# A mixture-of-experts pipeline over 66 of 68 slot tiles, the last two behind a branch

## The chip, the core and the metric

The kernel runs on one core of a Trainium2 chip. A core has five engines, each with its own stream of instructions: TensorE (PE, matrix products; its weight loads are shown apart as PEld), VectorE (DVE), ScalarE (ACT), GpSimd (POOL) and SyncE (SP), which here only issues transfers. ACT and POOL issue some transfers too. Sixteen DMA engines carry them between the chip's main memory and the core's on-chip memory (SBUF); products land in PSUM, a small accumulator memory in banks. Engines wait for each other by semaphores. The metric is the device time of one launch in microseconds (us); shorter is better.

## The reference

The input `x` has 2 sequences of 2048 tokens, 512 wide, all in float32. A normalized `xn` goes into causal attention with one head and into a mixture of experts (MoE); the result is `x + attention * silu(moe)`.

```python
xn = _layernorm(x)
s = attention(xn, qkv, o_proj, gamma, beta)      # normalizes again, causal softmax, + xn
# experts: 8 of them, each token uses its best 2
scores = xf @ gate_w.T + gate_b + bias
top_scores, top_idx = jax.lax.top_k(scores, 2)
gates = jax.nn.softmax(top_scores)
h = silu(xf @ w1[e].T + b1[e])                   # 512 -> 352
y = h @ w2[e].T + b2[e]                          # 352 -> 512
out = sum over the two experts of gate * y
x = x + s * silu(out)
```

There are 4096 tokens and so 8192 pairs of a token and an expert. How many of them each expert gets depends on the data.

## The kernel before

**Stages.** First the kernel folds the weights (`fold`), normalizes `x` block by block (`norm`, `keys`), and makes keys, queries and values, which it keeps in main memory. In the same stage `route` chooses the two experts of each token on VectorE. Then come the experts, tile by tile, and then attention, which gathers the experts' rows as it ends.

**Slots.** The experts work on slots of 128 rows, called tiles here. Each expert's tokens are laid out in halves of 64 rows; an expert with `n` tokens takes `n / 64` halves, rounded up. The number of tiles `NS` is fixed when the program is built, for the worst case that the data may bring: 8192 pairs and up to 63 rows of padding in each of 8 experts give 135 halves, so `NS` is 68. The first `FULL`, 60, are whole tiles of one expert each (52 of them in 26 pairs by `pair_step`, with fewer multiplications); the other 8 are half tiles, whose two halves may belong to different experts. `route` computes for each expert the halves that it uses, and sums them up over the experts in `behind`; its last element is the number of halves in use. Slots past that hold no pair. Nobody reads their rows of `y`, but the kernel computes them.

**One tile's chain.** For tile `i`: `gather` (POOL) reads the tile's rows of `zu_d` by index into `xs`; `turn` (a transposing transfer on SP) and `join` (DVE) make `xT`; `up` (PE) multiplies with `w1` into `ph`; `turn_h` scales it (ACT) into `h`, splits it (POOL) into `hu` and transposes it (SP) into `huT`; `join_h` (DVE, then ACT with the activation) makes `ht`; `down` (PE) multiplies with `w2` into `py`; `keep_y` copies it (DVE for these tiles) into one of two buffers `y` and stores it (SP) to the tile's rows of `y_d` in main memory. In a half tile PE works on 64 columns at a time, the two halves side by side; the second half's expert is copied into `w1c` (by ACT, `copy_w1`) and `w2c` (by DVE, `copy_w2`). Each such step reads an expert's number from SBUF into an engine's register.

**Order.** The order of the instructions on every engine is the order in which the program writes them, with no planner. `experts_step(i)` writes one step of the pipeline: the `y` of tile `i - 4`, the gather of `i + 6`, the transpose of `i + 4`, the join of `i + 1`, the up product of `i`, the down product of `i - 3`. The steps stretch over `i` from -5 to `NS + 4`. From step 59 on, each step also issues three parts of the list `early` on SP: 16 parts of the keys `k` and then 4 of the queries `q`, which the first scores of attention need, so the list ends in step 65. When it ends, POOL's `query_sums(0)` is written.

**Where experts end.** After step `NS - 1` the program writes:

```python
    copy_w2(NS - DOWN)
    for s in range(2):
        begin_scores(s)
    for j in direct(0):
        chunk_scores(0, j)
    for i in range(NS, NS + DOWN + 2):
        experts_step(i)
    st.close()
    wp.close()
```

`chunk_scores(0, j)` (PE, `ps`) is the first tile's work of attention, here between the last full step of the experts and the three down products that are left. `st.close()` and `wp.close()` give back the experts' buffers and weights; attention's own buffers are laid over them. Then the loop over attention's tiles begins: its first pass loads `v` (16 transfers on SP), makes `block_sums(0)` (`tk`, three parts on DVE and one on POOL), then the scores of the second tile (`ps`) and the products of `fast_scores` (`p`).

Of the kernel before, what the change touches and what calls it, by code (L numbers as in the profile page):

```python
# [12 lines left out]
I32 = mybir.dt.int32  # L13
# [7 lines left out]
P = 128  # L21
# [5 lines left out]
def gated_attention_moe(  # L27
# [28 lines left out]
    nc = tc.nc  # L56
    B, S, D = x.shape
    E, _, H = w1_t.shape
# [17 lines left out]
    FULL = (2 * NT * P - E * HALF) // P  # L76
    NS = -(-((2 * NT * P + E * (HALF - 1)) // HALF) // 2)
    NSP = NS + NS % 2
    NJ = FULL + 2 * (NS - FULL)
    assert HL < P and HL % 32 == 0 and D == 512 and TB == 512  # L80

# [19 lines left out]
    y_rows = y_d.rearrange("(n p) d -> p n d", p=P)  # L101

    const = ctx.enter_context(tc.tile_pool(name="const", bufs=1))
# [9 lines left out]
    share = [const.tile([P, 1, NT], F32, name=f"share{k}") for k in range(2)]  # L113
    toki = const.tile([P, NSP], I32, name="toki")
    eidi = const.tile([P, NJ], I32, name="eidi")
    b1sel = const.tile([P, NH, NJ], F32, name="b1sel")


# [46 lines left out]
    xin = {}  # L165
# [13 lines left out]
    nc.vector.memset(b1s, 0.0)  # L179
    gb = mp.tile([P, E, 1], F32, name="gb")  # L180
    gbias = mp.tile([P, E, 1], F32, name="gbias")

    def load_small():
        nc.sync.dma_start(out=gam, in_=gamma)
# [23 lines left out]
    def load_raw(c, pair):  # L208
        for i, queue in zip(pair, (nc.sync, nc.scalar)):

            cuts = (0, P, D) if c == 0 and i == 0 else (0, D)
            for at in (slice(*cut) for cut in zip(cuts, cuts[1:])):
                queue.dma_start(out=parts[i][:, c, at], in_=srcs[i][ts(c, P), at])
# [18 lines left out]
    def norm(b):  # L232
        norm_stats(b)
        norm_roots(b)
        norm_rows(b)
# [284 lines left out]
    def route():  # L520

        with ExitStack() as rt:
# [7 lines left out]
            for e in range(E):  # L530
# [5 lines left out]
                out=tri, in_=tri, compare_op=ALU.is_ge, fill=0.0,  # L536
# [105 lines left out]
            behind = rp.tile([P, 3, E, 1], F32, name="behind")  # L642
# [6 lines left out]

            shift = rp.tile([P, E, 1], F32, name="shift")
            nc.vector.scalar_tensor_tensor(
                shift, first[:, 0], float(HALF), excl[:, :, 0:1], ALU.mult, ALU.subtract
# [161 lines left out]
    load_small()  # L816
    for c in range(NK):
        load_raw(c, (2, 3))
    norm(0)
    fold(wqk, parts[0], parts[1], 1.0 / math.sqrt(KEY))  # L820
    keys(0)
# [59 lines left out]
    def gather(i):  # L881
        xs = xsp.tile([P, ZW], U16, name=f"xs_{i}", tag="xs")
        nc.gpsimd.indirect_dma_start(  # L883
            out=xs, out_offset=None, in_=zu_d,
            in_offset=bass.IndirectOffsetOnAxis(ap=toki[:, order[i] : order[i] + 1], axis=0),
        )
        xss[i] = xs
# [49 lines left out]
    DOWN = 3  # L937
# [13 lines left out]
    def turn(i):  # L951
        xh = xhp.tile([P, 2 * ND, P], U16, name=f"xhT_{i}", tag="xhT")
        nc.sync.dma_start_transpose(out=xh, in_=xss[i][:, : 2 * D])
        xhs[i] = xh

    def join(i):
        xT = xtp.tile([P, ND, P], F32, name=f"xT_{i}", tag="xT")
        nc.vector.tensor_copy(  # L958
            xT.bitcast(U16).rearrange("p c (t h) -> p c t h", h=2),
            xhs.pop(i).rearrange("p (h c) t -> p c t h", h=2),  # L960
        )
        xts[i] = xT
# [13 lines left out]
    def copy_w1(i):  # L976
        if i >= FULL:
            ev = expert(places(i)[1][1], mybir.EngineType.Activation)
            nc.scalar.copy(w1c, w1[0][:, bass.ds(ev, 1), :, :].rearrange("p o c h -> p (o c) h"))

    def copy_w2(i):
        if i >= FULL:
            ev = expert(places(i)[1][1], mybir.EngineType.DVE)
            for rows, c in ((P, slice(0, NH - 1)), (HL + 1, slice(NH - 1, NH))):
                nc.vector.tensor_copy(
                    w2c[:rows, c, :],
                    w2[:rows, bass.ds(ev, 1), c, :].rearrange("p o c d -> p (o c) d"),
                )

    def up(i):  # L990
        ev = experts[i] = expert(places(i)[0][1], mybir.EngineType.PE)
        xT = xts.pop(i)
        ph = ps_a.tile([P, TB], F32, name=f"ph_{i}", tag="a")[:, :H]
        for c in range(ND):
            rhs = [w1[0][:, bass.ds(ev, 1), c, :].rearrange("p o h -> p (o h)")]
            rhs += [w1c[:, c, :] for _ in places(i)[1:]]
            for k, (at, _) in enumerate(places(i)):
                nc.tensor.matmul(  # L998
                    ph[at, :], lhsT=xT[:, c, at], rhs=rhs[k],
                    start=(c == 0), stop=(c == ND - 1),  # L1000
                )
        phs[i] = ph
# [71 lines left out]
    def turn_h(i):  # L1074
        h = phs[i] if i in paired else hp.tile([P, H], F32, name=f"h_{i}", tag="h")
        nc.scalar.mul(h, phs.pop(i), xss.pop(i)[:, 2 * D : 2 * D + 2].bitcast(F32))
        hu = hus[i % NHU]
        nc.gpsimd.tensor_copy(  # L1078
            hu[:, :, :H], h.bitcast(U16).rearrange("p (d h) -> p h d", h=2)
        )  # L1080
        huT = hp.tile([P, 2 * NH, P], U16, name=f"huT_{i}", tag="huT", bufs=3)
        nc.sync.dma_start_transpose(out=huT, in_=hu.rearrange("p h d -> p (h d)"))
        huTs[i] = huT

    def join_h(i):
        ht = hp.tile([P, NH, P], F32, name=f"ht_{i}", tag="ht", bufs=3)
        nc.vector.tensor_copy(  # L1087
            ht.bitcast(U16).rearrange("p c (t h) -> p c t h", h=2),
            huTs.pop(i).rearrange("p (h c) t -> p c t h", h=2),
        )  # L1090
        for c, (h0, hn) in enumerate(HCH):
            for at, j in places(i):
                nc.scalar.activation(  # L1093
                    ht[:hn, c, at], ht[:hn, c, at], AF.Silu, bias=b1sel[:hn, c, j : j + 1]
                )
        hts[i] = ht

    def down(i):
        ht = hts.pop(i)
        ev = experts.pop(i)  # L1100
        py = ps_b.tile([P, D], F32, name=f"py_{i}", tag="b")
        for c, (_, hn) in enumerate(HCH):
            k = hn + 1 if c == NH - 1 else hn
            rhs = [w2[:k, bass.ds(ev, 1), c, :].rearrange("p o d -> p (o d)")]
            rhs += [w2c[:k, c, :] for _ in places(i)[1:]]
            for n, (at, _) in enumerate(places(i)):
                nc.tensor.matmul(  # L1107
                    py[at, :], lhsT=ht[:k, c, at], rhs=rhs[n],
                    start=(c == 0), stop=(c == NH - 1),
                )  # L1110
        pys[i] = py

    def keep_y(i, copy=nc.vector.tensor_copy):
        y = yp.tile([P, D], F32, name=f"y_{i}", tag="y")
        copy(y, pys.pop(i))  # L1115
        nc.sync.dma_start(out=y_rows[:, order[i], :], in_=y)
# [5 lines left out]
    def experts_step(i):  # L1122


        def at(f, k):
            if 0 <= i + k < NS:
                f(i + k)

        if i != NS:
            at(copy_w2, -DOWN)  # L1130
        if 0 <= i - DOWN - 1 < NS:
            keep_y(i - DOWN - 1, *[nc.scalar.copy] * (i < paired.start))
        if i >= 0:
            at(gather, FIRST)
        at(turn, 4)
        if i + 1 not in xts:
            at(join, 1)

        for _ in range((2, 2, 1, 4, 3, 3, 1)[i] if 0 <= i < paired.start else 0):
            w1_sums(*sums_left.pop(0))  # L1140
        if i < FULL:
            at(join_h, -2)
        at(up, 0)
        at(copy_w1, 1)
        at(turn_h, 0)
        if i >= FULL:

            at(join_h, -2)
        at(down, -DOWN)
# [165 lines left out]
    while w2_left:  # L1315
# [12 lines left out]
        out=keep, in_=keep, compare_op=ALU.is_ge, fill=-HUGE,  # L1328
        base=0, pattern=[[-1, P]], channel_multiplier=1,
    )  # L1330
    for i in range(NS):
        if i in paired:
            if (i - paired.start) % 2 == 0:
                pair_step(i)
            continue
        if i == paired.stop:

            pairs_st.close()
            right_st = lambda **k: right(reuse_waits="tile", **k)
            kp2 = right_st(st=att, name="kp2", bufs=NBB)  # L1340
            qp2 = right_st(st=att, name="qp2", bufs=NQ)
            sq = right_st(st=att, name="sq", bufs=1)


            wcp = right_st(st=st, name="wcp", bufs=1)
            w1c = wcp.tile([P, ND, H], F32, name="w1c")
            w2c = wcp.tile([P, NH, D], F32, name="w2c")
        experts_step(i)
        if i < paired.start:
            if i + 1 == paired.start:  # L1350
                join(i + 2)
                x_sums(i + 1)
        for _ in range(3):
            if i >= paired.stop and early:
                f, b, c = early.pop(0)
                f(b, c)
                if not early:
                    query_sums(0, nc.gpsimd)
    copy_w2(NS - DOWN)
    for s in range(2):  # L1360
        begin_scores(s)
    for j in direct(0):
        chunk_scores(0, j)
    for i in range(NS, NS + DOWN + 2):
        experts_step(i)
    st.close()
    wp.close()

# [471 lines left out]
```

## Time and profile before

| what | value |
|---|---|
| time, median of 3 runs | 1022.73 us (1021.96 to 1026.66) |
| the profiled execution's own time | 1024.79 us |
| its span, first to last instruction | 1023.1 us |
| busy: PE, DVE, POOL, ACT | 1013.5, 712.2, 482.1, 408.9 us |
| granted TensorE clock | 0.999 of full speed |
| half tiles: first up product, last down product starts | 525.4 us, 583.8 us |
| moved by DMA | 209.42 MB, mean 205 GB/s |

A line of the profile names an engine, the line of the kernel's file (L1107), the operation, the buffers written and read (`py<-arena,ht`), how many, and busy time, mean duration and the idle time before it with what ended it. In a listing by time the first number is the start in us from the span's start, the second the duration in us. A "q" behind an engine (SPq) means its queue of instructions that only issue transfers or handle registers. The chain that ended last is followed back from the last instruction: at each step to what released it, or to the instruction before it on its engine. Ends of matmuls are modelled, so a busy TensorE is not one at its peak.

### The profile page before, as it was taken

What the parts mean: (1) busy time and instruction counts of PE and PEld (TensorE: products, weight loads), DVE (VectorE), ACT (ScalarE), POOL (GpSimd) and SP (SyncE); (2) the same over time, 40 slices, a digit from 0 to 9 for tenths busy, and PEclk for the clock granted to TensorE, in tenths of its full rate; (3) what the DMA queues carried; (4) which work ended last, traced back from release to release, by engine and by line L of the source; (5) the groups of instructions that cost most, each with busy time, mean ns of one, the idle gap of its engine ahead of it and who ended that gap; (6) DMA issues with size and microseconds to landing.
All of it is one profiled execution on the core that took longest, in us unless ns stands there. A gap on an engine that the chain in (4) does not pass through costs nothing.

```text
span 1023.1 us, 13492 instructions
## 1 busy us (share of the span) xinstructions
PE 1013.5 (99%) x3956; PEld 666.2 (65%) x3956; DVE 712.2 (70%) x1395; ACT 408.9 (40%) x817; POOL 482.1 (47%) x479
## 2 busy tenths in 40 slices
PE   9999999999999999999999999999999999999998
PEld 4688888864666766676654447677675544447577
DVE  5777746896777777767734659778576556888667
ACT  3344445322454445444445222132345454542341
POOL 3364564003644444444431247164556776754272
PEclk9999999999999999999999999999999999999999
DMA  8799986989999999999999567454768769653371
GB/s 300 203 252 296 303 264 248 341 283 198 206 220 221 213 212 211 219 216 212 209 201 246 155 205 157 105 143 144 192 181 235 215 196 254 184 135 111 98 162 42
DMA packets 299367, 209.42 MB, mean 205 GB/s; under 512 B 234392, under 2 KB 247448, under 8 KB 298272
## 3 DMA queue, kind: packets, MB, share of 16 engines
q1 hardware_dynamic: 283840, 156.09, 61.7%
q0 software_dynamic: 10560, 35.17, 12.8%
q10 hardware_dynamic: 4896, 17.30, 4.6%
q8 instruction: 34, 0.56, 0.2%
q14 instruction: 37, 0.30, 0.1%
HBM read 92.89 MB, written 60.03 MB: 149 GB/s over the span
## 4 chain that ended last, share of the span: by engine, by line
PE 89%; DMA 4%; issue 3%; DVE 2%; POOL 1%; ACT 1%; SPq 1%; POOLq 0%; DVEq 0%; ACTq 0%
PE py L1107 15%; PE ps L1219 12%; PE p L1482 12%; PE p L1050 10%; PE p L1271 8%; PE po L1434 6%; PE bank_a L465 5%; PE bank_b L465 5%; PE bank_c L465 5%; PE p L1434 3%; PE bank_d L465 2%; PE ph L998 2%; DMA y_d<-y 1%; DMA raw<-in_qkv_t_dram 1%; PE pg L347 1%
## 5 line engine op out<-in xcount | busy, mean ns | idle before, releaser
L1107 PE MATMUL py<-arena,ht 128*128 (+3 forms) x408 | 182.3, 593 | 0.0
L1219 PE MATMUL ps<-k,q 128*128 128x512 f32 (+3 forms) x416 | 143.0, 495 | 0.0
L1394 POOL COPY pu<-pT 128x1024 uint16<-128x1024 uint16 (+2 forms) x74 | 82.5, 1147 | 119.4 <-ACT pT L1384 59.5
L1078 POOL COPY hu<-h 128x704 uint16<-128x704 uint16 x68 | 63.5, 953 | 154.6 <-issue 119.9
L1107 PEld LDWEIGHTS py<-arena,ht 128*128 128x128 f32 (+3 forms) x408 | 73.2, 183 | 82.1 <-issue 77.0
L1219 PEld LDWEIGHTS ps<-k,q 128*128 128x128 f32 x416 | 74.6, 190 | 66.8 <-issue 57.4
L883 POOL DMA_INDIRECT xs<-zu_d,toki x68 | 81.0, 1191 | 70.8 <-DVE toki L731 55.9
L1093 ACT ACTIVATE ht<-ht,b1sel 128x128 f32<-128x128 f32 (+3 forms) x228 | 71.1, 378 | 97.1 <-DVE ht L1087 97.1
L1057 DVE TENSOR_TENSOR h<-p,h 128x176 f32<-128x176 f32 x182 | 55.5, 337 | 60.8 <-PE p L1050 57.2
L1577 POOL DMA_INDIRECT yg<-y_d,posi x64 | 67.7, 1058 | 36.0 <-DVE yg L1588 20.5
L1434 PE MATMUL po<-v,pT 128*128 128x512 f32 x152 | 67.9, 593 | 0.4 <-DVE pT L1416 0.4
L280 POOL COPY zu<-z 128x1024 uint16<-128x1024 uint16 x32 | 37.5, 1173 | 61.3 <-DVE z L265 61.3
L1416 DVE COPY pT<-puT 128x1024 uint16<-128x1024 uint16 (+2 forms) x74 | 54.0, 757 | 10.3 <-DMA puT<-pu 10.2
L1384 ACT ACTIVATE pT<-pT,nm 128x1024 f32<-128x1024 f32 x14 | 16.1, 1148 | 110.2 <-DVE nm L1307 71.2
L1115 ACT COPY y<-py 128x512 f32<-128x512 f32 x55 | 32.2, 585 | 62.7 <-PE py L1107 48.1
L1384 ACT ACTIVATE pT<-ps,nm 128x512 f32<-128x512 f32 (+3 forms) x52 | 30.0, 581 | 64.5 <-DVE nm L1307 40.8
L1277 DVE TENSOR_TENSOR pT<-p,pT 128x512 f32<-128x512 f32 x49 | 32.9, 686 | 25.9 <-PE p L1271 22.2
L1434 PEld LDWEIGHTS po<-v,pT 128*128 128x128 f32 x152 | 28.5, 190 | 32.6 <-issue 30.9
L958 DVE COPY xT<-xhT 128x1024 uint16<-128x1024 uint16 x68 | 46.6, 709 | 4.3 <-DMA xhT<-xs 4.1
L1606 POOL TENSOR_TENSOR o<-o,yg 128x512 f32<-128x512 f32 x30 | 42.0, 1399 | 14.3 <-DVE o L1598 14.2
L1598 DVE SCALAR_TENSOR_TENSOR o<-xo,xscale,o 128x512 f32<-128x512 f32 x30 | 27.3, 918 | 28.7 <-ACT o L1595 28.7
L1087 DVE COPY ht<-huT 128x768 uint16<-128x768 uint16 x68 | 38.7, 569 | 10.3 <-DMA huT<-hu 10.2
(323 smaller groups left out, 2155.4 us busy)
## 6 DMA issues: line engine op xcount, KB each, us to landing
y_d<-y SPq DMA_DIRECT2D x68, 256.0 KB, 4.6
zu_d<-zu SPq DMA_DIRECT2D x32, 264.0 KB, 3.2
kt_d<-kT ACTq DMA_DIRECT2D x8, 1024.0 KB
k<-kt_d SPq DMA_DIRECT2D x32, 256.0 KB, 4.9
q<-qt_d SPq DMA_DIRECT2D x32, 256.0 KB, 5.3
v<-v_d SPq DMA_DIRECT2D x32, 256.0 KB, 4.7
xo<-in_x_dram SPq DMA_DIRECT2D x32, 256.0 KB, 4.0
x<-in_x_dram SPq DMA_DIRECT2D x30, 256.0 KB, 5.3
```

What stands on the lines that cost most here:

```text
L465: nc.tensor.matmul(ps[:, r, :], lhsT=lhs[:, c, ts(r, P)], rhs=rhs[:, c, :], start=(start and r + c == 0), stop=(c == 1), skip_group_check= ...
L883: nc.gpsimd.indirect_dma_start(out=xs, out_offset=None, in_=zu_d, in_offset=bass.IndirectOffsetOnAxis(ap=toki[:, order[i] : order[i] + 1], ...
L1050: nc.tensor.matmul(ps, lhsT=x[:, c], rhs=y(c).rearrange("p o h -> p (o h)"), start=(c == 0), stop=(c == ND // 2 - 1),)
L1078: nc.gpsimd.tensor_copy(hu[:, :, :H], h.bitcast(U16).rearrange("p (d h) -> p h d", h=2))
L1093: nc.scalar.activation(ht[:hn, c, at], ht[:hn, c, at], AF.Silu, bias=b1sel[:hn, c, j : j + 1])
L1107: nc.tensor.matmul(py[at, :], lhsT=ht[:k, c, at], rhs=rhs[n], start=(c == 0), stop=(c == NH - 1),)
L1219: nc.tensor.matmul(ps[:, :w], lhsT=aqs[seq[s] // 2][:, c, ts(t % 2, P)], rhs=aks[first + j][:, c, :w], start=(c == 0), stop=(c == ND - 1),)
L1271: nc.tensor.matmul(ps, lhsT=x[:, c], rhs=y[:, c], start=(c == 0), stop=(c == ND // 2 - 1))
L1394: nc.gpsimd.tensor_copy(pu[:, : 2 * w].rearrange("p (h d) -> p h d", h=2), turned[s][:, k : k + w].bitcast(U16).rearrange("p (d h) -> p h ...
L1434: nc.tensor.matmul(dst, lhsT=turned[s][:, ts(k, P)], rhs=avs[first + k // BT][:, k % BT, cols], start=(start and k == k0), stop=(k == k1 - 1),
L1482: nc.tensor.matmul(dst, lhsT=a[:, k], rhs=v(k), start=(k == 0), stop=(stop and k == n - 1))
L1577: nc.gpsimd.indirect_dma_start(out=y, out_offset=None, in_=y_d, in_offset=bass.IndirectOffsetOnAxis(ap=posi[k][:, n : n + 1], axis=0),)
```

## The change

The pipeline now runs over `NM = NS - 2`, 66 tiles. All four bounds that were `NS` in the expert steps are `NM`. Tiles 66 and 67 are written after the pipeline, each as a plain sequence of the ten steps of its chain, inside an `If`: the body runs when the number of halves in use exceeds `2 * NM`, 132. `route` copies that number as an integer to a new small tile, `used`, and every engine reads it into a register and branches on it. `fill_rows`, called early in the program, stores two blocks of `x` to the rows of `y_d` that belong to these two tiles, so that they hold something when the body is skipped.

```diff
+    NM = NS - 2
...
+    used = const.tile([P, 1], I32, name="used")
...
+    def fill_rows():
+        for k in range(NM, NS):
+            nc.sync.dma_start(out=y_rows[:, k, :], in_=xin[0][:, k - NM, :])
...
+            nc.vector.tensor_copy(used, behind[:, 2, E - 1])
...
     for c in range(NK):
         load_raw(c, (2, 3))
+    fill_rows()
     norm(0)
...
         def at(f, k):
-            if 0 <= i + k < NS:
+            if 0 <= i + k < NM:
                 f(i + k)
 
-        if i != NS:
+        if i != NM:
             at(copy_w2, -DOWN)
-        if 0 <= i - DOWN - 1 < NS:
+        if 0 <= i - DOWN - 1 < NM:
             keep_y(i - DOWN - 1, *[nc.scalar.copy] * (i < paired.start))
...
-    for i in range(NS):
+    for i in range(NM):
         if i in paired:
...
-    copy_w2(NS - DOWN)
+    copy_w2(NM - DOWN)
     for s in range(2):
         begin_scores(s)
     for j in direct(0):
         chunk_scores(0, j)
-    for i in range(NS, NS + DOWN + 2):
+    for i in range(NM, NM + DOWN + 2):
         experts_step(i)
+    n_used = nc.values_load(used[0:1, 0:1], min_val=0, max_val=2 * NS)
+    with tc.If(n_used > 2 * NM):
+        for i in range(NM, NS):
+            gather(i)
+            turn(i)
+            join(i)
+            copy_w1(i)
+            up(i)
+            turn_h(i)
+            join_h(i)
+            copy_w2(i)
+            down(i)
+            keep_y(i)
     st.close()
     wp.close()
```

## The prediction

> **What bounds the kernel now.** I read the page first, then the chain that ended last, then each engine in order of time around the change's place, the end of the experts (525 to 592 us).
>
> The page's busy row:
>
> ```profile
> PE 1013.5 (99%) x3956; PEld 666.2 (65%) x3956; DVE 712.2 (70%) x1395; ACT 408.9 (40%) x817; POOL 482.1 (47%) x479
> ```
>
> TensorE looks full, so two tiles fewer should be worth their matmuls. That is a mean over stages, so next comes the chain that ended last, in order of time, from 557 us (start us, us, what):
>
> ```profile
> 557.00 5.39 DMA y_d<-y
> 562.39 0.02 issue
> 562.42 0.69 DVE y L1115
> 563.11 0.61 DVE xT L958
> 563.72 0.04 issue
> 563.76 2.59 PE ph L998 x16
> 566.35 2.58 PE py L1107 x12
> 568.93 7.06 PE ps L1219 x16
> 575.99 8.42 PE py L1107 x36
> 584.41 6.21 PE ps L1219 x16
> ```
>
> Read backwards: the second score chunk (584.41) follows three down products (575.99), these follow the first tile's score chunks (568.93). Before 563.76 the chain leaves TensorE: the up product of tile 67 waits for `xT`, which stands on VectorE behind the copy of `y` of tile 62, which waits for the store of `y` of tile 60 to land (two `y` buffers). That store was issued only at 557.00, although its `y` was copied at 550.57 to 551.26. SyncE's queue was late. SP in order of time (start, us, line, what):
>
> ```profile
> 546.08 0.38 SPq L1116 DMA_DIRECT2D y_d<-y  x1
> 546.56 1.44 SPq L953 DMA_TRANSPOSE xhT<-xs  x1
> ...
> 551.68 1.50 SPq L953 DMA_TRANSPOSE xhT<-xs  x1
> ...
> 558.89 0.94 SPq L911 DMA_DIRECT2D k<-kt_d  x1
> 559.89 0.94 SPq L920 DMA_DIRECT2D q<-qt_d  x2
> ```
>
> SP carries, per tile, one `y` store, two transposes and three parts of the prefetch of keys and queries. The two `q` loads at 559.89 are the last things that the first score chunks need. GpSimd shows when they landed:
>
> ```profile
> 565.90 0.72 POOL L1238 TENSOR_TENSOR sq<-q 128x256 f32<-128x256 f32 x1 [8.22 <-DMA q<-qt_d]
> ```
>
> And the DMA engines are full there (window; busy by engine; clock, DMA share, GB/s):
>
> ```profile
> 535.00:545.00 10.00, 10.00 (x49) 4.00 (x49) 3.17 (x6) 5.47 (x13) 1.54 (x2) 1.00 1.31 204
> 545.00:555.00 10.00, 10.00 (x56) 5.02 (x54) 5.80 (x10) 5.80 (x17) 1.65 (x2) 1.00 1.08 283
> ```
>
> So up to about 557 the stage runs at TensorE's pace (half tiles start at 525.37, 530.66, 535.95, 541.24, 546.24, 552.0, 557.2, near 5.3 us apart, where ph and py alone are 2.59 + 2.58 = 5.17), but SP and the DMA engines follow close behind.
>
> [...]
>
> **The change part by part.**
>
> *Is the body skipped?* The reference's inputs give the experts 1037, 1102, 1013, 955, 1075, 976, 989 and 1045 of the 8192 choices; rounded up to halves of 64 that is 17+18+16+15+17+16+16+17 = 132. The test is "more than 132", so it is skipped. Expert 3 would need six more tokens to add a half.
>
> *Fill rows at the start.* Two stores of 256 KB on SP, each about 0.37 us to issue, at about 19.1 us, between the weights (17.25 to 19.10) and the `zu` stores (19.20). They wait for the first block of `x`, landed at 7.82 us. Behind them: the `zu` stores, then the load of block 2, which reuses the buffer read and so waits for the stores, some 4.6 us (the `y` row); issued about 24.5 instead of 21.5, landed about 30, read by VectorE at 37.99. SP's next work waits until 30.39 anyway. Cost 0; without that 8 us of cover, 3 us.
>
> *`used` copy.* One VectorE copy of 0.16 us (like `xscale`) in routing. TensorE runs without a gap over 226 to 251 us, so 0.
>
> *Removed, tiles 66 and 67.* On TensorE 2 x 5.17 = 10.3 us; between 557.0 (end of the down product beside tile 65) and 568.93, where the first score chunks start, lie these two steps and their stall: 11.9 us. On SP, transposes of `xs` 1.44 + 1.50 with gaps of 0.09, thus 3.1 us ahead of the `q` loads (the other four DMAs come after them). On POOL two gathers of 264 KB (526.4 and 530.9), copies `hu`; on ACT two w1 copies, `h`, the activations; on VectorE `xT`, `ht`, w2 copies, `y`: all off the chain once TensorE no longer waits there.
>
> *What is late next.* Without the two steps TensorE would start the score chunks at 557.0, but `q` landed at 565.8. The loads stay in step 64, and nothing is moved ahead for them. With 3.1 us less on SP they land at 562.7. Relief from the gathers and transposes can bring more; the floor is when the things ahead are ready: `h` of tile 64 at 551.62, `hu` to 552.5, its transpose to 553.9, three loads to 555.4, landing 5.4 later: 560.8. I take 561.7, so scores at 561.8 instead of 568.93: 7.1 us (ends 6.0 and 8.1). So some 4.8 us of the 11.9 become a new wait for `q`. The three down products behind keep their 8.42 us, since their waits on VectorE have the same order.
>
> *Register load and branch.* After the last down product each engine reads `used` into a register, and branches. The nearest row:
>
> ```profile
> L971 PEldq TENSOR_LOAD <-eidi x42: 295/357/1070, 243.1 to 559.7; - x42
> ```
>
> So 0.36 us on PE (to 1.07). [...] TensorE's sequencer runs ahead: that load at 559.7 serves tile 67, whose product starts at 563.76, and the last register operation of the down products was at 581.8, with the array busy to 584.4. So load and branch (about 0.5) fit under the last product. What the join costs is unknown[...]. If PE must run empty first, it restarts as at 584.34, where its weight loads stood 0.81 us before the first of `ps`; upper bound twice that, 1.6, lower bound 0. I take 0.7.
> Behind the branch: on VectorE `block_sums` (tk, 1.21 + 2.48 us, needed 9.5 us after the last down product, 593.89 against 584.41; slack 5); on POOL its part (2.34 us, before at 571.16, now after the join, since the buffers of the experts come free only there; needed 11 us after, so hidden); on SP the 16 loads of `v` (585.58 to 596.4, landing 5.9 later, first read at 612.46: slack 10 us); on ACT nothing for 8 us. So only TensorE's gap counts.
>
> *Sum.* 7.1 - 0.7 - 0.1 = 6.3 us. From 590 us on the chain is mostly TensorE's, so it carries to the end. The profiled execution took 1024.79 us, its span 1023.1, and 1.7 lie around it, unchanged; 1018.5 is what I expect of that execution. It stands 2.06 above the median, 1022.73, so 1016.4 for the median.
>
> **Rivals.**
> *A meeting of the engines at the branch.* All five wait for each other. The last is VectorE with the `y` copy (0.69), then SP with its store (0.4) and load and branch (0.5), then the signals there and back, ten steps of 0.05 (a semaphore step on PE takes 51 ns): 2.1 us, plus 0.7 to restart. Gain 4.2: about 1018.5. [...] Against: data waits suffice.
> *The join waits for the last `y` stores to land.* 0.69 + 0.4 + 4.6 + 0.5 + 0.7 = 6.9 us: gain 0.1, about 1022.6. With an instruction fetch on top, estimated at 1.0 (0.2% of 16 engines' span over 34 packets) to 4.6 (a store's landing), up to 1027. [...] Against: only SP and readers of `y` need them, and the first gather of `y` is at 614.2. To be slower by over 0.5% the branch must cost 12.3 us, so this needs several fetches in a row besides.
> *The branch is taken* (the change does not save what it says; slower). From 133 halves on both tiles run unpipelined: gather 1.2 + 5.0, transpose 1.4 + 4.6, `xT` 0.7, up 2.6, `h` 0.6, `hu` 0.8, transpose 1.4 + 4.6, `ht` 0.6, activation 1.5, down 2.6, `y` 0.7 = 28.3 us; the second, whose `xT` stands behind the first's `y` on VectorE, 16 more. Minus 6.3: about 1061. Against: the count above.
> *`q` is no limit.* The DMA relief pulls `q` in by 8 us: gain near 10.5, 1012. Against: the floor of 560.8.
>
> **How the numbers follow.** Likeliest case 0.62, its own range 1014.6 to 1017.6; meeting 0.16; landing wait 0.13, half of it above 1023; taken branch 0.03; `q` no limit 0.06. A difference under about 0.5% (5.1 us) can't be told from none by a measurement of this kernel: faster lies below 1017.6, slower above 1027.8. Faster: 0.62 less 0.06 at its edge, plus 0.06: 0.62. Slower: 0.03 and the landing wait's worst part, 0.06: 0.09. The rest, 0.29, is no difference. The range of 1014.0 to 1023.0 leaves out 0.06 below and about 0.10 above.
>
> **What the profile after would show.** Two gathers, two `y` stores and four transposes fewer, but two more `y` stores from `x` near 19 us; PE `ps` first at about 562, after a gap of some 5 us ended by DMA `q`; the three down products again 8.4 us; then a gap under 1.5 us before `ps` at about 578. A gap there of 3 us means the meeting, of 7 the landing wait; ph and py of tiles 66 and 67 after it would mean a taken branch. I am wrong if `q` lands at the old time, or the gap at the branch is over 2 us.

## The result, and the profile after

The kernel with the change took 1016.51 us in the median of 9 executions (1013.27 to 1019.85), the kernel before, on the same chip, 1022.99 (9 executions, 1021.96 to 1026.66). The ratio is 0.9935, with a 95% interval of 0.9916 to 0.9954: about 6.5 us, or 0.65%, faster. The prediction was 1016.4 us. The profiled execution of the change took 1013.27 us (span 1011.6) and was the lowest of its nine, while that of before (1024.79, span 1023.1) lay 1.8 us above its median. So the two profiles differ by 11.5 us where the medians differ by 6.5, and a part of what follows is about this difference.

The page's busy row of the changed kernel:

```profile
PE 1002.6 (99%) x3900; PEld 660.9 (65%) x3900; DVE 705.9 (70%) x1386; ACT 401.5 (40%) x801; POOL 473.0 (47%) x475
```

There are 56 products fewer on TensorE (3900 against 3956), which are the up and down products of two tiles, and it is busy for 10.9 us less. No instruction of tiles 66 and 67 was run. Where does the gain arise? From 21 us on, the starts of matching products of the two profiles agree within 0.02 us up to 548 us (in the first 21 us some differ by up to 0.65 us, which leaves no trace later), so the two stores of `fill_rows` and the copy of `used` cost nothing. What is left is the end of the experts. TensorE in order of time (as in the prediction: start us, duration us, what; in brackets the idle time before it and what ended it):

```profile
555.72 0.59 PE L1115 MATMUL py<-w2c,ht 97*64 97x512 f32 x1
557.91 7.11 PE L1227 MATMUL ps<-k,q 128*128 128x512 f32 x16 [1.60 <-issue]
...
573.73 6.25 PE L1227 MATMUL ps<-k,q 128*128 128x512 f32 x16 [0.30 <-PEq L1375]
```

The first score chunk starts at 557.91 instead of 568.93 us, 11.0 earlier, after a gap of 1.60 us. The second one, behind the three down products and the branch, starts at 573.73 instead of 584.41, 10.7 earlier. The difference of 0.3 is the gap at the branch. SyncE in order of time shows why the queries came so early:

```profile
546.99 1.22 SPq L1090 DMA_TRANSPOSE huT<-hu  x1
548.25 1.52 SPq L919 DMA_DIRECT2D k<-kt_d  x3
549.88 0.38 SPq L1124 DMA_DIRECT2D y_d<-y  x1
551.93 1.22 SPq L1090 DMA_TRANSPOSE huT<-hu  x1
553.20 0.57 SPq L919 DMA_DIRECT2D k<-kt_d  x1
553.82 0.94 SPq L928 DMA_DIRECT2D q<-qt_d  x2
554.86 0.41 SPq L1124 DMA_DIRECT2D y_d<-y  x1
```

In the kernel before, this queue issued one entry on the heels of the other, and `q` was issued at 559.89. Now it stands idle between a store and the next transpose (550.26 to 551.93): the backlog is gone, and `q` is issued at 553.82. The stores of `y` are early too: the two above are issued 2.0 and 2.1 us after their copies ended (547.84 and 552.78), against 5.7 for the one at 557.00 in the kernel before, and no wait for a store is left here. The DMA engines have a little more room (the same windows as in the prediction; the last three numbers are granted clock, DMA share and GB/s):

```profile
535.00:545.00 10.00, 10.00 (x49) 3.98 (x49) 4.46 (x8) 5.35 (x13) 1.55 (x2) 1.00 1.13 240
545.00:555.00 10.00, 10.00 (x60) 4.11 (x58) 5.61 (x9) 6.61 (x21) 2.82 (x3) 1.00 0.91 267
```

The shares fell from 1.31 and 1.08 to 1.13 and 0.91. GpSimd in order of time tells when the queries were all there, and when the branch was passed:

```profile
558.68 0.72 POOL L1246 TENSOR_TENSOR sq<-q 128x256 f32<-128x256 f32 x1 [3.46 <-DMA q<-qt_d]
...
573.66 2.35 POOL L1260 TENSOR_TENSOR tk<-k 128x1024 f32<-128x1024 f32 x1 [12.09 <-PEq L1375]
```

`sq` starts at 558.68 against 565.90. Its wait for `q` points to what ended TensorE's gap of 1.60 us, to which the list of TensorE puts only "issue"; the experiments below on the order of the loads show it. `tk` now stands behind the branch, as foreseen, and costs nobody time.

Last the branch itself. These are some of its instructions (durations in ns, least, median and greatest, then the start of the first and the last in us):

```profile
L1375 PEldq EVENT_SEMAPHORE  x2: 51/51/51, 573.5 to 573.6; - x2
...
L1375 POOLq COMPARE_BRANCH  x1: 45/45/45, 560.8 to 560.8; - x1
L1375 POOLq INC_SWDGE_SEM  x1: 1515/1515/1515, 561.8 to 561.8; - x1
...
L1375 ACTq COMPARE_BRANCH  x1: 45/45/45, 570.2 to 570.2; - x1
L1375 PEldq COMPARE_BRANCH  x1: 240/240/240, 571.8 to 571.8; - x1
L1375 DVEq COMPARE_BRANCH  x1: 72/72/72, 573.9 to 573.9; - x1
L1375 SPq COMPARE_BRANCH  x1: 53/53/53, 575.5 to 575.5; - x1
```

The engines pass it each at its own time: GpSimd at 560.8, ScalarE at 570.2, TensorE at 571.8, VectorE at 573.9, SyncE at 575.5. They don't meet. TensorE's sequencer branches while the array still works on the last down product, which ends at 573.43. Only the two semaphore steps at 573.5 and 573.6, of 51 ns each, come after it; what they are for the trace doesn't say. They leave the array idle for 0.30 us.

### The profile page after: what moved, and what is told of

It reads as the page before. It is cut to its first block, busy times and chain, and to the rows that moved or that the text cites. A ratio compares the mean times of both kernels' runs of the same rounds, so it can differ in the third digit from the quotient of the medians.

```text
span 1011.6 us, 13333 instructions
## 1 busy us (share of the span) xinstructions
PE 1002.6 (99%) x3900; PEld 660.9 (65%) x3900; DVE 705.9 (70%) x1386; ACT 401.5 (40%) x801; POOL 473.0 (47%) x475
## 5 line engine op out<-in xcount | busy, mean ns | idle before, releaser
L1115 PE MATMUL py<-arena,ht 128*128 (+3 forms) x396 | 176.7, 593 | 0.0
L891 POOL DMA_INDIRECT xs<-zu_d,toki x66 | 76.4, 1158 | 70.6 <-DVE toki L738 55.9
L1101 ACT ACTIVATE ht<-ht,b1sel 128x128 f32<-128x128 f32 (+3 forms) x216 | 68.0, 380 | 92.1 <-DVE ht L1095 92.1
L1628 POOL TENSOR_TENSOR o<-o,xo 128x512 f32<-128x512 f32 x30 | 43.2, 1439 | 2.4
```

Source lines behind the costliest of these rows:

```text
L891: nc.gpsimd.indirect_dma_start(out=xs, out_offset=None, in_=zu_d, in_offset=bass.IndirectOffsetOnAxis(ap=toki[:, order[i] : order[i] + 1], ...
L1101: nc.scalar.activation(ht[:hn, c, at], ht[:hn, c, at], AF.Silu, bias=b1sel[:hn, c, j : j + 1])
L1115: nc.tensor.matmul(py[at, :], lhsT=ht[:k, c, at], rhs=rhs[n], start=(c == 0), stop=(c == NH - 1),)
```

## The experiments

The theory: the two tiles' steps and their wait for `xT` leave TensorE, the loads of `q` come earlier because SyncE and the DMA engines have less to carry, and the rest of a wait for `q` remains; the branch costs little. The rivals: the gain is the work of the tiles alone and the transfers don't matter; the branch costs or brings something of itself; the two profiles differ by accident. The expectations were written down before each run.

**The change once more, unaltered.** No edit.

> The changed kernel once more, unaltered, to see what one execution's profile leaves out. Its first profiled execution took 1013.27 us and its span was 11.5 us shorter than before's, but the median of nine was only 6.5 us shorter. Theory (load timing): where the first score product starts varies from execution to execution with the landing of q; then a profile near 1016.5 us shows the gap ahead of it at 4 to 5 us instead of 1.6. Rival (clock): the granted clock falls for a few us in most executions (0.998 instead of 1.000 were listed); then the gap stays near 1.6 us and the loss of 2 to 6 us lies in a stretch at half clock elsewhere. Time 1014 to 1019 either way.

It took 1016.58 us (n = 6, 1014.05 to 1018.99), ratio 0.9936 (0.9915 to 0.9958). Neither expectation came true as written: the gap is neither 4 to 5 us nor 1.6, and the half clock that the rival looked for elsewhere follows the gap. Its profiled execution took 1016.66 us, right at the median, and is therefore the better witness of the usual case. TensorE in order of time:

```profile
559.59 8.80 PE L1227 MATMUL ps<-k,q 128*128 128x512 f32 x16 [2.43 <-issue]
...
577.11 6.25 PE L1227 MATMUL ps<-k,q 128*128 128x512 f32 x16 [0.30 <-PEq L1375]
```

The second score chunk starts 3.38 us later than in the other profile of the same kernel. Of these, 0.84 is a later last down product, 0.83 a longer wait (2.43 against 1.60), and 1.69 are the same 16 products, which took 8.80 instead of 7.11 us. The windows of this run (columns as above) say why:

```profile
557.00:560.00 3.00, 0.57 (x3) 0.30 (x2) 0.49 (x2) 0.00 (x0) 0.00 (x0) 1.00 1.23 301
560.00:563.00 3.00, 3.00 (x5) 1.32 (x4) 0.00 (x0) 0.00 (x0) 2.57 (x4) 0.52 0.81 210
```

Right after the gap the granted clock falls to half, for 3.41 us in all (from 560.1). A gap of 2.43 us was enough for that here, and one of 1.60 was not. The experiment that fills the gap, further down, says more on what counts.

How often does it happen? Of the 15 executions of the change in these two measurements, 11 had a mean granted clock of 0.998, with times of 1016.10 to 1019.85 us and a median of 1016.66. Four had 0.999 or 1.000, with times of 1013.27 to 1014.61. The first profile shows the rarer case. A mean clock over the execution doesn't tell where the half clock was; that it is at this place is shown in the profile of the second run only.

**Without the branch.** The register load, the branch and its body are removed. This kernel never computes tiles 66 and 67, which with these inputs hold no pair.

```diff
-    n_used = nc.values_load(used[0:1, 0:1], min_val=0, max_val=2 * NS)
-    with tc.If(n_used > 2 * NM):
-        for i in range(NM, NS):
-            gather(i)
...
-            keep_y(i)
```

> The changed kernel without the register load, the branch and its body (tiles 66 and 67 are never computed; with these inputs no pair lies in them). Theory (the join costs TensorE next to nothing): same time as the change within 0.5 us; the gap ahead of the second score chunk is 0.0 to 0.1 us instead of 0.30. Rival (the branch costs several us elsewhere, on VectorE, GpSimd or SyncE, which the profile of one execution hides): 2 to 5 us faster than the change.

1016.05 us (n = 22), ratio 0.9932 (0.9916 to 0.9948). The gap before the second chunk is gone:

```profile
559.08 8.55 PE L1227 MATMUL ps<-k,q 128*128 128x512 f32 x16 [2.61 <-issue]
...
575.98 6.28 PE L1227 MATMUL ps<-k,q 128*128 128x512 f32 x16
```

The branch is worth 0.5 us in the medians, within the uncertainty of both, and 0.30 in the traces. This execution too has a gap above 2.4 us followed by slow products (8.55 us).

**The branch alone.** The kernel before, all 68 tiles in its pipeline, with the copy of `used` and behind the pipeline the branch with its body, which is skipped.

```diff
+    NM = NS - 2
...
+    used = const.tile([P, 1], I32, name="used")
...
+            nc.vector.tensor_copy(used, behind[:, 2, E - 1])
...
+    n_used = nc.values_load(used[0:1, 0:1], min_val=0, max_val=2 * NS)
+    with tc.If(n_used > 2 * NM):
+        for i in range(NM, NS):
+            gather(i)
...
+            keep_y(i)
```

> The kernel before, all 68 tiles in the pipeline, and behind it the branch of the change, whose body would compute tiles 66 and 67 a second time and is not run. Theory (the join costs next to nothing): the time of before within 1 us, with a gap of about 0.3 us at the join. Rival (the branch costs 2 us or more, hidden in the change by the two tiles): 2 to 5 us slower than before.

1023.22 us (n = 22), ratio 1.0002 (0.9991 to 1.0012); the gap before the second chunk is the same 0.30 us. So the branch neither costs nor brings anything measurable, and the whole gain belongs to the 66 tiles.

```profile
567.13 7.13 PE L1222 MATMUL ps<-k,q 128*128 128x512 f32 x16
```

This profiled execution took 1022.95 us, near its median, and shows something of the kernel before too: at the end of the experts TensorE goes through all 68 tiles without a wait, the last two tiles' products fill 557.15 to 567.13, and the stall ahead of tile 67 in the profile of before (1.40 us of idle array) isn't there.

**The transfers kept.** The gathers and the first transposes of tiles 66 and 67 stay in the pipeline. Everything else of the change is as it was: no products, copies or stores of these tiles.

```diff
-        def at(f, k):
-            if 0 <= i + k < NM:
+        def at(f, k, end=NM):
+            if 0 <= i + k < end:
                 f(i + k)
...
-            at(gather, FIRST)
-        at(turn, 4)
+            at(gather, FIRST, NS)
+        at(turn, 4, NS)
...
-            gather(i)
-            turn(i)
             join(i)
```

> The change, with the two gathers and the first two transposes of tiles 66 and 67 left in the pipeline, and only the rest of the two tiles behind the branch. Theory (these transfers held up SP and the DMA engines, and their removal, not only that of the matmuls, moved q from 565.8 to 558.6 us): q lands at 561 to 565 us, TensorE waits 4 to 8 us for it, and the time is 3 to 7 us above the change. Rival (SP was late for other reasons, such as the y stores or the activations of tiles 66 and 67): q lands before 559.5 us and the time is that of the change within 1 us.

1023.75 us (n = 22, 1021.01 to 1028.09), ratio 1.0002 (0.9989 to 1.0016). The whole gain is gone, although TensorE has the products of two tiles less to do. Its waits (total us, times, longest), and the place in order of time:

```profile
PE ps L1227 <- DMA q<-qt_d: 6.8, 1, 6.8
```

```profile
563.19 9.97 PE L1227 MATMUL ps<-k,q 128*128 128x512 f32 x16 [6.76 <-DMA q<-qt_d]
...
581.88 6.25 PE L1227 MATMUL ps<-k,q 128*128 128x512 f32 x16 [0.30 <-PEq L1375]
```

The loads of `q` are issued at 558.05 instead of 553.82, and TensorE waits 6.76 us for them. Then it runs at half clock (windows of this run):

```profile
558.00:565.00 7.00, 1.81 (x2) 0.84 (x3) 0.00 (x0) 0.20 (x1) 1.00 (x2) 0.55 1.06 237
565.00:569.00 4.00, 4.00 (x6) 1.69 (x5) 0.00 (x0) 0.00 (x0) 1.81 (x3) 0.50 0.29 91
569.00:580.00 11.00, 11.00 (x41) 4.72 (x41) 6.57 (x12) 3.09 (x12) 0.00 (x0) 1.00 0.13 48
```

The half clock lasts 10.24 us here, three times 3.41. Against the first profile of the change the second chunk is 8.15 us later: 5.28 from the start of the first chunk and 2.86 from its slow products. By the medians the change lost 7.2 us, just above the expected 3 to 7, which had no term for the clock; the profiled execution (1021.30) was one of the lower ones of its 22. The theory of the transfers is shown: without their removal the tiles' work on TensorE turns into waiting.

**The gathers alone kept.** Of the edit above only that of the gathers, so that `turn` stays in the body.

```diff
-            at(gather, FIRST)
+            at(gather, FIRST, NS)
...
-            gather(i)
             turn(i)
```

> The change with only the two gathers of tiles 66 and 67 left in the pipeline (264 KB each on GpSimd's queue), their transposes behind the branch. With gathers and transposes left in, q was issued at 558.05 instead of 553.82 us and the first score product started at 563.2 instead of 557.9. Theory of the prediction (SP's own time for the two transposes, 3.1 us, is the larger part; the gathers are the smaller): q issued at 554.5 to 556, first score product at 558.5 to 560.5, time 0 to 3 us above the change. Rival (the gathers load the DMA engines and stretch all other transfers, so they are the larger part): q issued after 556, first score product after 561, 3 us or more above the change.

1017.08 us (n = 5, 1016.43 to 1022.20), ratio 0.9930 (0.9906 to 0.9954): 0.6 us above the change, within its uncertainty. The profiled execution was the longest of the five and had lost 3.7 us before this place, so its trace says little on the size. In it `q` is issued at 559.24, 3.7 less of which is 555.6, within the expected range, but the wait for `q` is 4.59 us and the first chunk takes 9.37. By the medians the gathers are the smaller part of the 7.2 us, though the intervals leave room for some 3 us; the rest comes with the two transposes, which stand in SyncE's own queue ahead of `q`. The transposes without the gathers were not run, since they need the gathered rows.

**The queries first.** In the change, only the order of the prefetch list: the keys and queries of the first tile's scores come first. Nothing is added or removed.

```diff
-    early = [(fetch_k, b, c) for b in range(NBB) for c in range(ND)]
-    early += [(fetch_q, n, c) for n in range(NQ) for c in range(2)]
+    early = [(fetch_k, b, c) for b in (2, 3) for c in range(ND)]
+    early += [(fetch_q, 0, c) for c in range(2)]
+    early += [(fetch_k, b, c) for b in (0, 1) for c in range(ND)]
+    early += [(fetch_q, 1, c) for c in range(2)]
```

> The change with the 20 prefetch parts in the order of use: keys 2 and 3, the first queries, keys 0 and 1, the second queries (as many transfers, same steps). Theory (a late q leaves TensorE idle for 1.6 to 2.8 us, and in most executions the idle time makes the clock fall to half for a window of 3.41 us, which costs 1.7 us more): no gap ahead of the first score chunk, no half clock but at the end, and 2 to 5 us less than the change: about 1011 to 1013 us, with less spread. Rival (the half clock has nothing to do with the gap, and the spread comes from elsewhere): the gap goes, half clock and spread stay, 1.5 to 2.5 us less than the change at most.

1012.55 us (n = 5, 1012.13 to 1014.83), ratio 0.9892 (0.9870 to 0.9913). SyncE issues the two loads at 540.92 and 544.25 us, and TensorE goes on without a gap and at full clock:

```profile
557.88 7.13 PE L1229 MATMUL ps<-k,q 128*128 128x512 f32 x16
...
573.73 6.25 PE L1229 MATMUL ps<-k,q 128*128 128x512 f32 x16 [0.30 <-PEq L1377]
```

The same kernel was measured again among the last runs:

> The change with the prefetch in the order of use once more, beside the filler on the same chip. Theory (no wait, so no half clock): 1012 to 1015 us, 1 to 2 us below the filler's lower group, whose extra products take 1.7 us of which the wait hides most.

1013.85 us (n = 6, 1012.26 to 1016.62), ratio 0.9901 (0.9880 to 0.9922), again with no gap before the first chunk. Of the 11 executions of this kernel ten had a mean granted clock of 1.000 and one 0.999. Their median is 1013.28 us, 3.2 below that of the 15 executions of the change (not on the same chip; by the ratios to the kernel before it is 3.5 to 4.5): about the wait (1.6 to 2.4) and the half clock (1.7) together. This version beats both kernels. The interval of the first of its two measurements lies just below that of the change, that of the second overlaps it.

**The transfers kept, the queries first.** The fourth kernel's edit and this order together.

> Gathers and first transposes of tiles 66 and 67 left in the pipeline, as in the run that lost the whole gain, but with the prefetch in the order of use (queries third of five groups instead of last). Theory (the transfers cost time only because they make q late): most of the loss returns, 1012 to 1015 us, no wait for q over 1 us. Rival (the transfers also delay y stores, keys and transposes, and with them the steps): still 1019 us or more.

1014.21 us (n = 6, 1012.00 to 1016.76), ratio 0.9912 (0.9893 to 0.9932). TensorE doesn't wait for `q`:

```profile
558.95 7.13 PE L1229 MATMUL ps<-k,q 128*128 128x512 f32 x16
```

Of the transfers' 7.2 us (1023.75 against 1016.51) nothing measurable is left: 0.4 us above the second measurement without them, 1.7 above the first. They cost time only because `q` stood behind them.

**The order in the kernel before.** The same four lines in the kernel before.

> The kernel before with only the prefetch in the order of use, all 68 tiles in the pipeline. There q landed at 565.8 us and was used at 568.93, and the stage waited for y stores. Theory (q is not what the kernel before waits for): within 1 us of before. Rival (the order of the prefetch is worth time by itself): 3 us or more faster than before.

1024.57 us (n = 14), ratio 1.0008 (0.9997 to 1.0019). The profiled execution was the slowest of the fourteen (1026.24). Its waits of TensorE still have the old one, now ahead of tile 66:

```profile
PE ph L1000 <- DVE xT L960: 1.6, 1, 1.6
```

With 68 tiles `q` is not what ends last. In this execution the up product of tile 66 waits, behind a store of `y`; in that of the branch alone TensorE waits for nothing at this place. So the order is worth some 3 us only once the tiles are gone. The two steps do not simply add.

**The branch taken.** The test is changed so that 132 halves pass it, and the body runs.

```diff
-    with tc.If(n_used > 2 * NM):
+    with tc.If(n_used > 2 * NM - 1):
```

> The change with the test one half lower, so that the 132 halves of these inputs take the branch and tiles 66 and 67 are computed behind it, unpipelined. The prediction's rival gives 28.3 us for the first tile and 16 for the second, 44 us above the change, about 1061 us. If the body overlaps more than that estimate allows (gathers and transposes of the second tile beside the first), 25 to 35 us above it.

1058.46 us (two executions, 1057.28 and 1059.63), ratio 1.0336 (1.0304 to 1.0368), so 42 us above the change; between the profiles 44.0 (1055.6 against 1011.6). Its waits of TensorE:

```profile
PE py L1115 <- ACT ht L1101: 12.5, 3, 6.7
PE ph L1006 <- DVE xT L966: 10.8, 2, 6.0
```

The body's chain is laid bare, and of its up and down products most run at half clock (0.79 us each for up, against 0.46). The sum of the prediction's rival fits, its parts less: the first tile takes 23.4 us (to the end of its `y` copy at 598.3, from the last down product at 574.9) instead of 28.3, since GpSimd, past the branch early, issues its gather already at 563.19, beside the down products, and the second takes 20.2 instead of 16. That is the price in a launch whose data fill 133 halves.

**Filling the gap.** Two products that nobody reads are written ahead of the first chunk, so that TensorE is not idle while it waits for `q`.

```diff
+    fill = ps_a.tile([P, TB], F32, name="fill", tag="a")
+    for _ in range(2):
+        nc.tensor.matmul(fill, lhsT=ident, rhs=w2[:, 0, 0, :], start=True, stop=True)
     for j in direct(0):
         chunk_scores(0, j)
```

> The change with two needless products of 512 columns (about 1.7 us of matmuls, result unread) ahead of the first score chunk, where TensorE waits for q. q is as late as before. Theory (idle time lowers the clock): idle time shrinks to about 1 us or nothing, the clock stays whole, and although TensorE does more work the kernel is 1 to 2 us faster than the change, near 1015 us or below. Rival (only q's lateness counts): the time of the change, or up to 0.5 us more.

> The two needless products ahead of the first score chunk once more, since the first time its six executions fell into two groups (1014.5 to 1014.8, 1017.7 to 1020.4) and the one profiled was slow for another reason, a stall near 290 us. Theory (idle time lowers the clock): no half clock after the wait for q, and the lower group again near 1014.6. If the half clock comes after it all the same, keeping TensorE busy is not what keeps the clock.

1016.22 us (n = 6, 1014.50 to 1020.35), ratio 0.9925 (0.9900 to 0.9949), and in the second measurement 1017.02 (n = 6, 1015.20 to 1020.10), ratio 0.9933 (0.9912 to 0.9955). Neither is apart from the change. The trace of the second:

```profile
561.84 1.98 PE L1372 MATMUL fill<-arena,ident 128*128 128x512 f32 x4
564.45 7.11 PE L1227 MATMUL ps<-k,q 128*128 128x512 f32 x16 [0.63 <-PE fill L1372]
```

At this place the filler did what was meant: from the end of the last down product (561.9) to the first score lie 2.5 us, as in the second run of the change (2.43), but the 16 products then take 7.11 us, not 8.80, and the clock stays full. The first filler trace shows the same. From the last down product to the second chunk both take 18.4 us, against 20.0 in the second run of the change. That the fall of the clock follows from the idle array, and not from the time or the transfers, is thus seen in both.

In the times the expected 1 to 2 us below the change did not appear; by them alone the rival fits as well, and the first measurement's lower group, 1014.5 to 1014.8, did not come back. Both profiled executions (1020.35 and 1019.88) lost 5 to 6 us elsewhere, near 290 us. One transpose of `xs` takes 4.7 and 5.7 us of SyncE's queue there, against 2.5 in the first profile of the change, TensorE waits 2.20 and 2.17 us, and a half clock of 3.41 us follows here too. Why the transpose took so long was not found.

All the traces together tell more about what counts. In each of the 14, every stretch of full or half clock that ends within the execution is a whole number of steps of 3.41 us (the full clock of 1017.17 us in the profile of before is 298 of them, that of 1006.93 in the first of the change 295), so the trace can be cut into such windows. The time that TensorE was idle within one window at full clock, and the clock of the next:

| profile | window, us | idle, us | next |
|---|---|---|---|
| the change, first | 555.03 to 558.45 | 1.60 | full |
| the branch taken | 555.73 to 559.14 | 1.77 | full |
| filler, second, near the end | 1012.88 to 1016.29 | 1.97 | full |
| without the branch | 555.17 to 558.59 | 2.12 | half |
| filler, second, near 290 us | 289.25 to 292.67 | 2.17 | half |
| filler, first, near 290 us | 292.24 to 295.66 | 2.20 | half |
| the change, again | 556.69 to 560.10 | 2.43 | half |

No window at full clock in the 14 traces goes against this: up to 1.97 us idle the clock stayed, from 2.12 us on it fell. The gap with the branch taken is 2.01 us long, but 0.24 of it lies in the next window. Whether it was spared by that or by its length can't be told from these runs.

## Why the prediction was right or wrong

The number was right, 1016.4 against 1016.51, and so was the mechanism: two tiles' work leaves TensorE, `q` comes earlier but becomes the next wait, and the branch costs little. Several terms of the sum were mis-sized or missing, and that they cancel to 0.1 us is luck.

*The body is skipped.* Right; and since the body runs when the test is one half lower, the halves in use are just the 132 that were counted.

*Fill rows and the `used` copy cost nothing.* Right: from 21 us on the starts agree within 0.02 us up to 548 us, and the branch alone with the copy gave 1.0002.

*The two tiles and their stall leave TensorE.* Right: all of that stretch is gone, and the wait for `xT` with it. The stretch was taken too long. The down product beside tile 65 ended at 557.23 us, not at 557.0, which makes it 11.7; and 1.40 of that was a stall which the profile of the branch alone, near its median, doesn't have. There the two tiles fill 10.0 us.

*The three down products keep their 8.42 us.* Right: from the end of the first chunk (565.0) to the end of the last product (573.4) it is 8.4.

*`q` is what is late next.* Right in kind: the order with the queries first takes exactly this wait away, and gains 3 us. Wrong in size: the step "a new wait of some 4.8 us". Measured were 1.6 and 2.4 us in the two profiles. The floor of 560.8 us was too high. In it, `h` of tile 64 was set at 551.62, its time in the kernel before; with less on SyncE it was ready at 550.71. The transpose was done at 553.15 instead of 553.9 and the loads were issued by 554.76 instead of 555.4. The landing was put at 5.4 us after that, the duration of the loaded stage; GpSimd had all of the `q` that it needs (558.68) after 3.9. And TensorE started 0.8 us before that, at 557.91. So the first chunk came 9.3 to 11.0 us earlier, not 7.1. How much the relief of the gathers would bring was the author's estimate; kept alone, they took 0.6 us by the medians. The error of method: the floor was built from times of a stage whose load the change itself removes.

*The missing term.* The prediction had the wait cost its own length. An idle array of 2.4 us also brought the half clock, which cost 1.7 us in the profile at the median. Wait and clock together are 4.1 us there, close to the 4.8 that the wait alone was given. The closeness of the result rests on this too.

*The sum.* Between the profile of before (1024.79) and the second of the change (1016.66) lie 8.1 us, where 6.3 were foreseen for this pair. In the traces they are 9.3 at the first chunk, less 1.7 of half clock and 0.3 at the branch, thus 7.3 at the second chunk, and 0.8 after it. The medians differ by 6.5 only, since that profile of before lay 1.8 above its median. Its stall ahead of tile 67 is probably a part of these 1.8. Counted from the profile of the branch alone, the first chunk comes 7.5 us earlier (567.13 to 559.59): 10.0 of the two tiles, less a wait of 2.4. Less the half clock of 1.7 it is 5.9 at the second chunk. So the prediction removed some 2 us too many and left out 1.7 of clock; against that it gave the new wait 2.4 us too many and the branch 0.4. The 0.1 in its sum belongs to no term that it names, and its worst landing wait, 1027, ends below the 1027.8 from which it counts a part of that case as slower.

*The branch costs 0.7.* A little high: 0.30 in the traces, nothing measurable in the two kernels made for it. The 0.5 us for load and branch was the author's estimate: a row of before shows 0.36 of load, and none shows a branch. In the first profile of the change TensorE's load took 0.31 us and its compare-and-branch 0.24 (45 to 72 ns on the other four engines), and both lie under the last products (571.4 to 572.0, against 573.43).

*What lies behind the join is hidden.* Right for GpSimd's part and SyncE's loads. The first sum of VectorE's part of `tk` took 2.60 us instead of 1.21 and was hidden all the same (see below).

*The rivals.* Meeting of the engines: false, they pass at 560.8 to 575.5, each alone. Waiting for the last stores: false on TensorE; the gap is 0.30. That an instruction fetch may come on top there was the author's assumption and was not shown: the pages of before and after count the same 34 and 37 packets in the two queues of kind "instruction". Taken branch: not so here; its price was right in sum, 44 worked out, 44.0 between the profiles and 42 between the medians, while its two parts (28.3 and 16 against 23.4 and 20.2) were not. `q` no limit, 1012: not so for the change, but this is the time (1012.55 and 1013.85) of the kernel in which the order of the prefetch makes it so.

What stays open: why the wait is 1.6 us in one execution and 2.4 in another (the first chunk starts 4.09 and 4.93 us after the issue of `q`, so it is the transfers that take longer), whether the clock falls by the length of a gap or by its share of a window (between 1.97 and 2.12 us idle nothing was seen), and what makes the transposes near 290 us slow.

## What to carry to other kernels

Work out what is removed on every queue, not only on the engine that looks full: here two transposes in SyncE's queue, with the gathers that feed them, decided whether two tiles of matmuls less were worth 6.5 us or nothing. When a wait for a load becomes the next limit, look first at the order of the loads in the queue, which costs nothing to change; here it gave another 3 us, and before the change it would have given none. And price a wait of TensorE above some 2 us at more than its length: here, from 2.12 us idle within one step of 3.41 us on, the clock fell to half, and the 16 products after the wait took 1.4 to 2.9 us more.

## What the runs showed of the hardware that was not expected

The half clock after short gaps: 3.41 us of it after gaps of 2.17, 2.20, 2.43 and 2.61 us, 6.83 after 4.59 and 10.24 after 6.76; none after 1.60 and 2.01. At the first score chunk it cost 1.4 to 2.9 us. It comes and goes in steps of 3.41 us, and one step with 2.12 us of idle array was enough.

VectorE's `tk` beside that of GpSimd, in the first profile of the change (VectorE in order of time):

```profile
574.49 2.60 DVE L1260 TENSOR_TENSOR tk<-k,k 128x1024 f32<-128x1024 f32 x1 [0.33 <-DVEq L1375]
577.12 1.23 DVE L1260 TENSOR_TENSOR tk<-k,tk 128x1024 f32<-128x1024 f32 x1
```

The first of these sums took 1.21 us in the kernel before (from 585.05), where GpSimd's sum of the same kind was long over (571.16 to 573.50). Now GpSimd's runs from 573.66 to 576.01, and VectorE's, begun in that time, takes 2.60 us and ends 1.08 us after it. The two sums behind it take 2.49 us together, as before (2.48). So it was the one beside GpSimd's that took twice its time; by what, and whether it would again, one trace doesn't show. It cost nothing here: VectorE's last sum ends at 579.61, and the first product that reads `tk` starts at 583.25.

The compare-and-branch took 45 to 72 ns on ACT, GpSimd, SyncE and VectorE, and 240 ns on TensorE, in the first profile of the change. The skipped branch, with all five engines in it, left TensorE idle for 0.30 us there, in the second, and in the branch alone.
